# A state-space block in four layers: B, C and the step sizes of a segment out of one projection instead of two

## The chip, the cores and the metric

The kernel runs on one core of one Trainium2 chip. The metric is the time of one execution on the device, in microseconds (us); 19,610.8 us is the median of three runs of the kernel before. Engines are named as in the profile: PE is TensorE (PEld its weight loads), DVE is VectorE, ACT is ScalarE, POOL is GpSimd, SP is the engine from which all transfers (DMAs) are issued.

## The reference, cut to what matters

Four images of 64x64 tokens with 96 channels pass through four layers, each a mixer and a feed-forward part with a residual each. The mixer of layer 0 is a gated recurrence. Those of layers 1 to 3 are selective scans, and the change concerns them alone. For each image and layer:

```python
x_dbl = jnp.einsum('bkdl,kcd->bkcl', xs, x_proj_weight)        # k: 4 orders, d: 192 channels
dts, Bmat, Cmat = jnp.split(x_dbl, [DT_RANK, DT_RANK + D_STATE], axis=2)   # 6, 16 and 16 rows
dts = jnp.einsum('bkrl,kdr->bkdl', dts, dt_projs_weight)
delta = jax.nn.softplus(dts + dt_projs_bias[None, :, :, None])
# for each state n of 16, along the 4096 tokens:
dA = jnp.exp(dl[..., None] * A)
h = dA * h + (dl * u_l)[..., None] * b_l[:, :, None, :]
y = jnp.einsum('bkdn,bkn->bkd', h, c_l)
```

B, C and the step sizes (`dts`) of a token are three slices of one matrix product of the scan's input with `x_proj_weight`. The 4096 tokens are scanned in four orders: by rows and by columns, each forwards and backwards.

## The kernel before, in words

**Stages.** After layer 0, 12 stages follow: layers 1 to 3, and in each the four images. A stage takes one image through one layer's scans: 2 directions x 4 segments of 1024 tokens (T) x 3 chunks of 128 channel rows (two orders share a chunk, 64 partitions each) x 16 states n. One (chunk, state) of one segment is a **scan tile**; a segment has 48 tiles, a stage 384, the whole 4608. Positions below are given as chunk (first, second, third) and tile n (0 to 15), or as the tile's number in its stage.

**One scan tile** (`scans`, from line 873). ACT makes `da` = exp(delta x A). PE spreads row n of B over the channel rows by multiplying `bs` with a selector (`b_rows`, line 917: `bc<-bs,sel`, two matmuls into one of two double PSUM banks). DVE multiplies `bc` by `du`, in place in PSUM, and scans (`scan`, line 926). POOL multiplies the result `h` by the C row (`times_c`, line 948); the C row was read from DRAM by a DMA that repeats it over 64 partitions (`c_rows`, line 901: `c<-cs`, issued two tiles ahead). PE sums over the states (`add_quarters`, line 953: `acc<-c,twice`, eight matmuls) three tiles later. Each engine works through its instructions in the order in which the program issues them; the class `InOrder` records that order, which is why every instruction of the profile carries line 78.

**B in three parts.** `bs` is bf16 with 96 partitions: 0 to 31 hold B rounded to bf16, 32 to 63 the rounded remainder, 64 to 95 what the second rounding leaves. The selector adds up the three.

**Preparing a segment** (`prepare_segment`, line 775; 96 times). For each half k of 512 tokens, three matmuls (one per chunk of `u`) project onto 108 rows in one PSUM bank, `x_proj_b`: three copies of the 32 rows of B (two orders x 16 states) and, from row 96 on (NB3), the 12 rows of step sizes. ACT copies the step sizes to `rows` and casts all 96 B rows to `bs`; DVE subtracts `bs` from the bank into `rows[0:96]`; ACT casts the remainder to partitions 32 to 63 and 64 to 95 of `bs`. When both halves are done, POOL makes the last part in one instruction. After that the C rows are projected by themselves, again three matmuls per half, into a bank `x_proj_c`; ACT copies each to `rows[0:32]`, and SP stores them to `cs` in DRAM, where `c_rows` finds them.

**The planner.** Beside the scan tiles, three kinds of work are laid into the program as generators ("chains"), each `yield` ending a turn:

- the chunk chain, `prepare_chunk` of the next chunk (line 824): four passes over `dt_proj` banks, softplus on ACT and POOL; it starts at n = 0 of each chunk;
- the segment chain, `next_segment` (line 863): load `u`, wait two turns, then `prepare_segment` for the next segment; it starts at n = 4 of the second chunk;
- the jobs (`Job`, line 717; `between`, line 623): what lies between two layers for the next stage's image, namely the joining of the four orders, the output projection, the feed-forward part, the input projection and the convolution, in eight strips each.

Each scan tile gives one turn to the chunk chain, then one to the segment chain, and then as many turns to the job as its credit allows (1.65 per tile, line 1317; 2.6 for the last layer's jobs). These turns are issued between a tile's multiply and its scan (`beside`, line 1033). A turn that needs a PSUM bank announces it (`yield True`), and `pump` (line 136) refuses it when neither of the two single banks is free; a bank counts as free again from the next tile on. At n = 13 what is left of a chain is run out. A job that is not done at tile 356 of its stage (line 1022) is run out there with no scans beside it.

The weights of both projections lie in one array, XPW columns for each direction and chunk (lines 40 and 297); `_scan` fills it on the host (lines 1365 to 1376).

Of the kernel before, what the change touches and what calls it, by code (L numbers as in the profile page):

```python
# [15 lines left out]
ALU = mybir.AluOpType  # L16
# [5 lines left out]
NS = 16  # L22
DI = 192
R = 6
HID = 4 * C
T = 1024
MM = 512
# [9 lines left out]

NB3 = 96
NC2 = 2 * NS
XPW = NB3 + 2 * R + NC2  # L40
W_IN = 0
W_OUT = W_IN + 6 * 128
W_CW = W_OUT + 2 * C
# [5 lines left out]
W_XP = W_LN + 4  # L49
W_SSM = W_XP + 6 * XPW  # L50

# [48 lines left out]
def metaformer(ctx: ExitStack, tc: tile.TileContext, x, l0_ab, l0_rest, ssm, ffn, out):  # L100
    nc = tc.nc
    pe, act, dve, pool, sp = (
        InOrder(tc, e) for e in (nc.tensor, nc.scalar, nc.vector, nc.gpsimd, nc.sync)
    )
# [6 lines left out]
    def sb(bufs, tag, shape, dtype=F32):  # L111
        return pools[bufs].tile(shape, dtype, tag=tag, name=tag)

    def const(name, shape, dtype=F32):
        return pools[1].tile(shape, dtype, name=name)
# [9 lines left out]
    def bank(name):  # L125
        banks["free"] -= 1
        return banks["pool"].tile([128, MM], F32, tag="ps", name=name)

    def release():
        banks["back"] += 1  # L130
# [31 lines left out]
    for k in range(2):  # L162
        p = slice(64 * k, 64 * k + 64)
# [31 lines left out]
    for layer in range(4):  # L195
# [8 lines left out]
        b = const(f"b_{layer}", [128, 3 + C])  # L204
# [72 lines left out]
    class Weights:  # L277
# [17 lines left out]
        def load_xp(self):  # L295
            if self.xp is None:
                self.xp = sb(1, "xp", [128, 6 * XPW])
                sp.dma_start(out=self.xp, in_=ssm[self.layer - 1, :, W_XP:W_SSM])
# [476 lines left out]
    def prepare_segment(item, sg):  # L775

        xp = weights[item.layer].xp
        m = NB3 + 2 * R

        def project(ps, a, b, k):  # L780

            for c in range(3):
                o = (3 * item.d + c) * XPW
                cols = slice(k * MM, (k + 1) * MM)
                pe.matmul(
                    ps[0 : b - a],
                    xp[:, o + a : o + b],
                    sg.us[c][:, cols],
                    start=c == 0,
                    stop=c == 2,  # L790
                )
                if c:
                    yield

        sg.rows = sb(1, "rows", [128, T])
        for k in range(2):
            cols = slice(k * MM, (k + 1) * MM)
            ps = bank("x_proj_b")
            yield from project(ps, 0, m, k)

            bs = sg.bs[:, cols]
            act.copy(sg.rows[NB3:m, cols], ps[NB3:m])
            sg.steps = k == 1
            act.copy(bs, ps[0:NB3])
            yield
            rem = sg.rows[0:NB3, cols]
            dve.tensor_tensor(rem, ps[0:NB3], bs, ALU.subtract)
            release()
            yield
            for p in (32, 64):  # L810
                act.copy(bs[p : p + 32], rem[p : p + 32])
            yield k == 0
        pool.tensor_tensor(sg.bs[64:96], sg.rows[64:96], sg.bs[64:96], ALU.subtract)
        for k in range(2):
            cols = slice(k * MM, (k + 1) * MM)
            yield True
            ps = bank("x_proj_c")
            yield from project(ps, m, m + NC2, k)
            act.copy(sg.rows[0:NC2, cols], ps[0:NC2])
            release()  # L820
        yield
        sp.dma_start(out=sg.cs, in_=sg.rows[0:NC2])

    def prepare_chunk(item):

# [37 lines left out]
    def next_segment(items):  # L863

        sg = load_segment(items[0])
        for i in items:
            i.sg = sg
        yield
        yield
        yield True  # L870
        yield from prepare_segment(items[0], sg)

    def scans(stages, jobs, pac):
# [11 lines left out]
        for i in items[:3]:  # L885
            i.sg = sg
        drain(Chain(prepare_segment(items[0], sg), True))
        drain(Chain(prepare_chunk(items[0]), True))
        tiles = [(i, n) for i in items for n in range(NS)]
# [417 lines left out]
    with tc.tile_pool(name="pbig", bufs=2, space=bass.MemoryType.PSUM) as wides_pool:  # L1307
        wides.append(wides_pool)
        with tc.tile_pool(name="pl0", bufs=1, space=bass.MemoryType.PSUM) as pl0:
            gated(images, Job(between(images[0], 0), 2.6, patience=1), pl0)  # L1310
        stages = [(im, layer) for layer in range(1, 4) for im in images]
        jobs = []
        for at in range(len(stages)):
            jobs.append([])
            if at + 1 < len(stages):
                im, layer = stages[at + 1]
                jobs[-1].append(Job(between(im, layer - 1), 1.65))

            for im in {10: images[:2], 11: images[2:3]}.get(at, ()):
                jobs[-1].append(Job(between(im, 3, im.dst), 2.6))  # L1320
        with tc.tile_pool(name="pac", bufs=1, space=bass.MemoryType.PSUM) as pac:
            scans(stages, jobs, pac)
# [31 lines left out]
def _chunks(v):  # L1354

    v = v.reshape(2, 2, DI, -1)
    v = [np.concatenate([v[:, o, c : c + 64] for c, o in halves], 1) for halves in CHUNKS]
    return np.stack(v, 1).transpose(2, 0, 1, 3)


def _scan(in_w, conv_w, conv_b, xp_w, dt_w, dt_b, A_logs, Ds, ln_w, ln_b, out_w):
    w = np.zeros((128, W_SSM), np.float32)
    twice = np.r_[128:DI, 128:DI]

    xp = np.zeros((128, 2, 3, XPW), np.float32)
    m = NB3 + 2 * R
    for d in range(2):
        for chunk, halves in enumerate(CHUNKS):
            for k, (ch, order) in enumerate(halves):
                t = xp_w[2 * d + order].T[ch : ch + 64]  # L1370
                v = xp[64 * k : 64 * k + 64, d, chunk]
                for s in range(3):
                    v[:, 32 * s + NS * order : 32 * s + NS * order + NS] = t[:, R : R + NS]
                v[:, NB3 + R * order : NB3 + R * order + R] = t[:, :R]
                v[:, m + NS * order : m + NS * order + NS] = t[:, R + NS :]
    w[:, W_XP:W_SSM] = xp.reshape(128, -1)
    t = in_w.T
    w[:C, W_IN : W_IN + 448] = np.concatenate([t[:, :128], t[:, twice], t[:, DI:]], 1)
    dt = np.zeros((2 * R, 2, 3, 128), np.float32)
    for d in range(2):  # L1380
        for chunk, halves in enumerate(CHUNKS):
            for k, (ch, order) in enumerate(halves):
                t = dt_w[2 * d + order].T
                dt[R * order : R * order + R, d, chunk, 64 * k : 64 * k + 64] = t[:, ch : ch + 64]
    w[NB3 : NB3 + 2 * R, W_IN:W_OUT] = dt.reshape(2 * R, -1)
    w[:, W_OUT : W_OUT + C] = out_w.T[:128]
    w[:64, W_OUT + C : W_CW] = out_w.T[128:]
    taps = conv_w.reshape(DI, 9)
    w[:, W_CW : W_CW + 9] = taps[:128]
    w[:64, W_CW + 9 : W_CB] = np.concatenate([taps[128:, 0:3], taps[128:, 6:9]], 1)  # L1390
    w[64:, W_CW + 9 : W_CW + 12] = taps[128:, 3:6]
    w[:, W_CB:W_DTB] = np.stack([conv_b[:128], conv_b[twice]], 1)
    w[:, W_DTB:W_AL] = _chunks(dt_b[..., None]).reshape(128, -1)
    w[:, W_AL:W_DS] = _chunks(A_logs.reshape(4, DI, NS)).reshape(128, -1)
    w[:, W_DS:W_LN] = _chunks(Ds.reshape(4, DI, 1)).reshape(128, -1)
    w[:, W_LN : W_LN + 2] = np.stack([ln_w[:128], ln_b[:128]], 1)
    w[:64, W_LN + 2 : W_XP] = np.stack([ln_w[128:], ln_b[128:]], 1)
    return w
# [46 lines left out]
```

## Time and profile before

| | |
|---|---|
| median of three runs | 19,610.8 us (19,587.3 to 19,634.2) |
| profiled execution | 19,605.7 us; span of its instructions 19,603.9 us |
| mean granted TensorE clock | 0.816 of full speed |
| layer 0 and start | to 1802 us of the span |
| scan tiles | 1802 to 19,384 us |
| six C matmuls' group `x_proj_c`, 1152 in all | 657.8 us of PE, 687 ns mean |
| copies of C out of PSUM, 192 | 107.5 us of ACT, 560 ns mean |
| subtract `rows<-x_proj_b,bs`, 96x512, 192 | 130.1 us of DVE, 677 ns mean |
| `cs<-rows` stores, 96 | 4.6 us to landing (median) |

How to read it: a group's line names line, engine, operation, output<-inputs, shapes and count, then busy time and the mean of one, then the idle time of that engine just before these instructions and what ended most of it. `DVE bc <- PE bc` in the waits means that DVE stood before an instruction writing `bc` until PE's instruction writing `bc` was done. Busy shares of different engines overlap in time.

### The profile page before, as it was taken

To read this page: it belongs to the slowest core of one execution; us is meant where nothing else is said; L and a number is where in the kernel's file an instruction comes from. 1 tells how busy PE (TensorE), PEld (TensorE's weight loads), DVE (VectorE), ACT (ScalarE), POOL (GpSimd) and SP (SyncE) were. 2 spreads that over 40 slices of the span, in tenths; PEclk is the share of its full clock that TensorE was granted. 3 is DMA by queue.
4 is the path that set the end of the run, shared out by engine and by line. 5 is a ranking of instruction groups with operands and counts; after the bars stand their busy time and mean duration, and the time that the engine had idled before them with its cause. 6 is when DMAs were issued, how large, how long until landed. Compare 5 with 4: busy or idle time off the path is not lost. (4 is left out here: it accounts for less than half of the span.)

```text
span 19603.9 us, 224830 instructions
## 1 busy us (share of the span) xinstructions
PE 16279.3 (83%) x70400; PEld 4745.4 (24%) x70400; DVE 17669.3 (90%) x13768; ACT 12248.8 (62%) x19341; POOL 15496.4 (79%) x10086
## 2 busy tenths in 40 slices
PE   8998787787888888887888887887888888888877
PEld 3332121121122222222222222222222222223223
DVE  6757999999999999999999999999999999998885
ACT  4544665665665665675665665665675665666665
POOL 3435888888888888888888888888888888888886
PEclk9998786787787787797797797797797797797776
DMA  2213666676666666667666667666666666676664
GB/s 52 50 47 89 166 184 168 168 188 166 169 186 172 170 182 180 167 185 182 169 183 180 167 182 183 167 182 182 168 186 178 168 185 176 171 185 171 168 177 115
DMA packets 1269876, 3192.65 MB, mean 163 GB/s; under 512 B 440336, under 2 KB 440560, under 8 KB 1262544
## 3 DMA queue, kind: packets, MB, share of 16 engines
q1 hardware_dynamic: 1268688, 3178.27, 61.6%
q8 instruction: 568, 9.31, 0.2%
q14 instruction: 620, 5.08, 0.1%
HBM read 2818.81 MB, written 308.28 MB: 160 GB/s over the span
## 5 line engine op out<-in xcount | busy, mean ns | idle before, releaser
L78 POOL TENSOR_TENSOR c<-h,c 128x1024 f32<-128x1024 f32 (+1 forms) x4992 | 11332.9, 2276 | 3284.9 <-DVE h L78 1396.4
L78 DVE TENSOR_TENSOR_SCAN h<-da,carry,bc 128x1024 f32<-128x1024 f32 x4608 | 10797.5, 2343 | 598.7 <-POOL c L78 80.8
L78 PE MATMUL acc<-c,twice 64*64 64x512 f32 x36864 | 6246.6, 755 | 57.4 <-POOL c L78 57.4
L78 ACT ACTIVATE da<-delta,decay 128x1024 f32<-128x1024 f32 x4608 | 5280.8, 1148 | 1372.5 <-DVE h L78 1359.7
L78 DVE TENSOR_TENSOR bc<-du,bc 128x1024 f32<-128x1024 f32 x4608 | 5567.1, 1208 | 417.8 <-PE bc L78 389.6
L78 PE MATMUL bc<-bs,sel 96*128 96x512 bf16 x9216 | 3398.6, 457 | 2393.3 <-DVE h L78 2296.6
L78 ACT COPY carry<-h 128x1 f32<-128x1 f32 x3456 | 649.1, 188 | 2997.7 <-DVE h L78 2992.8
L78 PEld LDWEIGHTS <-sel 96*128 96x128 bf16 x9216 | 557.0, 101 | 7376.4 <-DVE h L78 5607.2
L78 PEld LDWEIGHTS acc<-c,twice 64*64 64x64 f32 x36864 | 1131.3, 153 | 2848.4 <-issue 1927.6
L78 ACT ACT_TABLE_LOAD x1165 | 1494.7, 1283 | 36.3 <-DVE mv L78 20.0
L78 PE MATMUL conv<-pad,tap_lo 128*128 128x512 f32 x1728 | 913.5, 639 | 0.6 <-ACT zh L78 0.6
L78 PE MATMUL dt_proj<-rows,w 12*128 12x512 f32 x1152 | 829.5, 807 | 6.3 <-ACT delta L78 6.3
L78 ACT ACTIVATE du<-e,ones 128x1024 f32<-128x1024 f32 x576 | 659.4, 1145 | 202.9 <-POOL delta L78 197.8
L78 POOL TENSOR_TENSOR delta<-delta,du 128x1024 f32<-128x1024 f32 x288 | 679.2, 2358 | 121.7 <-ACT du L78 121.3
L78 PE MATMUL x_proj_c<-u,xp 128*32 128x512 f32 x1152 | 657.8, 687 | 133.2 <-ACT rows L78 125.0
L78 PE MATMUL x_proj_b<-u,xp 128*108 128x512 f32 x1152 | 696.1, 722 | 53.7 <-ACT u L78 12.8
L78 ACT COPY y<-acc 128x1024 f32<-128x1024 f32 x288 | 291.3, 1012 | 713.8 <-PE acc L78 708.9
L78 POOL TENSOR_TENSOR e<-e,du 128x1024 f32<-128x1024 f32 x288 | 679.7, 2360 | 2.4 <-ACT du L78 2.4
L78 POOL TENSOR_TENSOR du<-delta,u 128x1024 f32<-128x1024 f32 x288 | 680.0, 2361 | 0.1
L78 POOL TENSOR_TENSOR delta<-delta,e 128x1024 f32<-128x1024 f32 x288 | 678.7, 2357 | 0.1
L78 ACT ACTIVATE c<-c,l_bias 128x512 f32<-128x512 f32 x384 | 263.6, 686 | 662.6 <-PE c L78 659.8
L78 PE MATMUL conv<-pad,tap_hi 128*128 128x512 f32 (+1 forms) x1152 | 598.8, 621 | 3.8 <-ACT u L78 3.8
(152 smaller groups left out, 15323.9 us busy)
## 6 DMA issues: line engine op xcount, KB each, us to landing
c<-cs SPq DMA_DIRECT2D x9216, 256.0 KB, 4.2
u<-u SPq DMA_DIRECT2D x288, 512.0 KB, 6.8
y<-y SPq DMA_DIRECT2D x1152, 128.0 KB, 3.5
y<-y SPq DMA_DIRECT2D x144, 512.0 KB, 6.4
xr<-x SPq DMA_DIRECT2D x224, 192.0 KB, 5.1
u<-u SPq DMA_DIRECT2D x288, 128.0 KB, 2.7
pad<-y SPq DMA_DIRECT2D x288, 128.0 KB, 5.1
z<-zl SPq DMA_DIRECT2D x96, 256.0 KB, 3.4
```

What stands on the lines that cost most here:

```text
L78: ins = f(*a, **k).ins
```

## The change

One projection per half in place of two. Its 108 rows are now: B (0 to 31), C (32 to 63), 32 rows of zero weights (64 to 95), and the step sizes at 96 to 107 as before. ACT copies all 108 rows to `rows` and casts only 32 rows of B to `bs`. DVE subtracts those 32 rows of `bs` from the bank's first 32 and writes the remainder to `rows[64:96]`. ACT casts the remainder twice, as before. SP's store of C now reads `rows[32:64]` and is issued right after the second half, ahead of POOL's subtract. The second loop with its two banks is gone. The job rate goes from 1.65 to 1.6 turns per tile.

```diff
-XPW = NB3 + 2 * R + NC2
+XPW = NB3 + 2 * R
...
-        sg.rows = sb(1, "rows", [128, T])
+        rows = sg.rows = sb(1, "rows", [128, T])
         for k in range(2):
             cols = slice(k * MM, (k + 1) * MM)
-            ps = bank("x_proj_b")
-            yield from project(ps, 0, m, k)
-
+            ps = bank("x_proj")
+            for c in range(3):
+                o = (3 * item.d + c) * XPW
+                pe.matmul(
+                    ps[0:XPW], xp[:, o : o + XPW], sg.us[c][:, cols], start=c == 0, stop=c == 2
+                )
+                if c:
+                    yield
             bs = sg.bs[:, cols]
-            act.copy(sg.rows[NB3:m, cols], ps[NB3:m])
+            act.copy(rows[0:XPW, cols], ps[0:XPW])
             sg.steps = k == 1
-            act.copy(bs, ps[0:NB3])
+            act.copy(bs[0:32], ps[0:32])
             yield
-            rem = sg.rows[0:NB3, cols]
-            dve.tensor_tensor(rem, ps[0:NB3], bs, ALU.subtract)
+            rem = rows[64:96, cols]
+            dve.tensor_tensor(rem, ps[0:32], bs[0:32], ALU.subtract)
             release()
             yield
             for p in (32, 64):
-                act.copy(bs[p : p + 32], rem[p : p + 32])
+                act.copy(bs[p : p + 32], rem)
             yield k == 0
-        pool.tensor_tensor(sg.bs[64:96], sg.rows[64:96], sg.bs[64:96], ALU.subtract)
-        for k in range(2):
-            cols = slice(k * MM, (k + 1) * MM)
-            yield True
-            ps = bank("x_proj_c")
-            yield from project(ps, m, m + NC2, k)
-            act.copy(sg.rows[0:NC2, cols], ps[0:NC2])
-            release()
-        yield
-        sp.dma_start(out=sg.cs, in_=sg.rows[0:NC2])
+        sp.dma_start(out=sg.cs, in_=rows[NC2 : 2 * NC2])
+        pool.tensor_tensor(sg.bs[64:96], rows[64:96], sg.bs[64:96], ALU.subtract)
...
-                jobs[-1].append(Job(between(im, layer - 1), 1.65))
+                jobs[-1].append(Job(between(im, layer - 1), 1.6))
...
-                for s in range(3):
-                    v[:, 32 * s + NS * order : 32 * s + NS * order + NS] = t[:, R : R + NS]
+                v[:, NS * order : NS * order + NS] = t[:, R : R + NS]
+                v[:, NC2 + NS * order : NC2 + NS * order + NS] = t[:, R + NS :]
                 v[:, NB3 + R * order : NB3 + R * order + R] = t[:, :R]
-                v[:, m + NS * order : m + NS * order + NS] = t[:, R + NS :]
```

## The prediction

> **What bounds the kernel now.** I read the page's busy lines first, then the groups of instructions.
>
> ```profile
> PE 16279.3 (83%) x70400; PEld 4745.4 (24%) x70400; DVE 17669.3 (90%) x13768; ACT 12248.8 (62%) x19341; POOL 15496.4 (79%) x10086
> ...
> PEclk9998786787787787797797797797797797797776
> ```
>
> ```profile
> L78 DVE TENSOR_TENSOR_SCAN h<-da,carry,bc 128x1024 f32<-128x1024 f32 x4608 | 10797.5, 2343 | 598.7 <-POOL c L78 80.8
> L78 DVE TENSOR_TENSOR bc<-du,bc 128x1024 f32<-128x1024 f32 x4608 | 5567.1, 1208 | 417.8 <-PE bc L78 389.6
> ...
> L78 PE MATMUL x_proj_c<-u,xp 128*32 128x512 f32 x1152 | 657.8, 687 | 133.2 <-ACT rows L78 125.0
> L78 PE MATMUL x_proj_b<-u,xp 128*108 128x512 f32 x1152 | 696.1, 722 | 53.7 <-ACT u L78 12.8
> ```
>
> DVE is the bound: each of 4608 scan tiles costs it one multiply (1208 ns) and one scan (2343 ns), 16,365 us in all, and the tiles run from 1802 to 19,384 us of the span. The change leaves those two alone. What can be won is DVE's idle time there. From the trace I took the distance from each multiply to the next and subtracted DVE's own other work between them. An undisturbed tile then takes about 3.56 us (1.208 + 2.343 and the seams), and all that lies above 3.56, over all tiles, is **429 us**. That is the most that any change of waits can bring. The waits say who causes it.
>
> ```profile
> DVE bc L78 <- PE bc L78: 389.6, 271, 5.1
> ...
> PEld x_proj_c L78 <- ACT rows L78: 157.9, 67, 4.9
> ...
> PE x_proj_c L78 <- ACT rows L78: 125.0, 65, 4.5
> ```
>
> Columns: total us, times, longest. The multiply waits for its operand `bc` from TensorE, 390 us in all. TensorE works in order, and the third projection (`x_proj_c`) is where it stands before ScalarE. The timeline of one case (columns: start us, duration, engine):
>
> ```profile
> 8635.58 0.56 ACT L78 COPY rows<-x_proj_c 32x512 f32<-32x512 f32 x1
> ...
> 8636.19 1.90 PE L78 MATMUL x_proj_c<-u,xp 128*32 128x512 f32 x4 [2.00 <-ACT rows L78]
> ...
> 8639.08 1.09 PE L78 MATMUL acc<-c,twice 64*64 64x512 f32 x8
> ...
> 8640.10 0.61 PE L78 MATMUL bc<-bs,sel 96*128 96x512 bf16 x2
> ...
> 8640.75 1.23 DVE L78 TENSOR_TENSOR bc<-du,bc 128x1024 f32<-128x1024 f32 x1 [1.41 <-PE bc L78]
> ```
>
> ScalarE comes late to empty a C bank (it had a table load and two passes of the next chunk's softplus ahead of it); TensorE stands 2.00 us; the matmuls behind it move back; DVE idles 1.41 us.
>
> To price this by place I summed the excess over 3.56 us by position in a segment (three chunks of 16 tiles). In tiles 2 to 9 of the three chunks it is 1.75, 0.47 and **1.91 us per segment** (96 segments); the other 24 positions together have 0.35. The C projection lies in tiles 2 to 8 of the third chunk. The first chunk's 1.75 holds 12 intervals at the starts of stages, where POOL waits up to 10.77 us for a `c<-cs` load behind the big loads of a new job; without them it is 1.68.
>
> **What the Trainium skill says.** "VectorE: DVE Perf Modes", section "Two Vector instructions with no wait between them": a Vector instruction whose output starts in another group of 32 partitions than the last output into that memory starts only after all earlier ones have finished. The trace agrees: of the four 64-partition COPYs that build `twice`, the second and fourth start 77 and 82 ns before the end of the one ahead; the third, which moves to partition 64, starts 13 ns after it. "TensorE: Matmul & The Clock Gate", section "LDWEIGHTS (loading the stationary operand)": a load's time goes with its columns; the medians agree, 175 ns for 108 and 109 ns for 32, while the matmuls take 594 and 593 ns. So 108 columns in one projection cost what 108 do now. Same page, Part 1: the clock falls to half after an idle window. The trace has half clock in 37% of the tiles, but 11% in tiles 4 to 7 of the third chunk, where C keeps TensorE busy.
>
> **The change, part by part**, for 96 segments.
>
> *Removed: six C matmuls, two ScalarE copies (558 ns each), two bank uses and seven turns of the segment's chain.* TensorE loses 658 us and ScalarE 107 us of busy time; neither counts as such, only what DVE waits. In tiles 2 to 9 of the third chunk the 1.91 us become what a chunk has with softplus and job but no C. The two neighbours are the nearest rows: 0.47 and 1.68. I take their mean, 1.08: (1.91 - 1.08) x 96 = **-80 us**. The ends are 0.47 (-138 us) and 1.68 (-22 us). The cover is not free: a bank that C does not hold goes to a job. By following the planner's rule (one turn of each chain per tile, a turn refused when no bank is free) through the code, counting turns and no times, jobs take 244 banks in those tiles now and 299 after, against 294 in the first chunk now. That is why I do not take 0.47. The half clock that a less busy TensorE gets is inside this substitution too.
>
> *The subtract, 192 of it, now reads partitions 0 to 31 and writes 64 to 95.* Its row is 96x512 at 677 ns; with 512 elements per partition as before I take 677 ns again. But it changes the output's partition group, and so does the scan behind it (`h` starts at 0). Now the subtract starts 91 ns before the multiply's end and the scan 80 ns before the subtract's. Each becomes +13 ns by the COPY row: 104 + 93 = 197 ns, x192 = **+38 us**, straight on DVE. It can't be a gain: the same elements, one instruction for one. Lower end 0, if none is held; upper end +54, if it also takes as long as DVE's slowest 512-element row with a PSUM operand (759 ns; 82 ns x192 = 16 us). It must now follow the rows copy as well, but waits for the later cast anyway (45 us in 17 waits now, the scan queued behind): no new wait.
>
> *The rows copy takes 108 partitions instead of 12, the cast 32 instead of 96*: 579 and 582 ns for 12 and 96 partitions now, so 0. The two casts of the remainder (616 ns) and POOL's 2124 ns subtract stay, in the same turn.
>
> *The `cs` store is issued about seven turns earlier and ahead of POOL's subtract.* SP's queue is in order; the store waits only for the two rows copies, some turns old by then, and the first reader is issued at tile 14 of the third chunk, so nothing waits for it: 0. Were the copy late, the `c` loads queued behind it would wait, and then POOL; they are issued two tiles ahead.
>
> *The first segment is prepared before any scan, uncovered.* ScalarE's first `e` starts at 1783.01 us, and its last cast before that ends at 1780.37; without C it can follow it: **-3 us**. The smaller `xp` load (648 columns for 840) saves at most part of the one 9 us wait for it: 0 to -2, taken as 0.
>
> *The job rate 1.65 to 1.6.* The count of turns puts the job's last step at tile 289 (stages 0 to 2), 345 (3 and 7) and 337 (the others), and the trace has the `u` stores there, at 290, 345 and 338. The deadline is tile 356: a job not done by then is run out with the scans standing. With both edits the last step comes at 298, 339 and 328, so there is no run-out; refused turns fall from about 165 to 103 per stage. In the last stage three jobs end at tile 333 instead of 373. The work is the same: 0. But every job step now meets other scan steps. Stages 4, 5, 6, 8 and 9 have one schedule and excesses of 22.7 to 36.2 us, so a new schedule may well move a stage by 5 us, and eight stages alike: +-40 us, for the range.
>
> **Sum:** -80 + 38 - 3 = **-45 us** on the profiled execution's 19605.7 (span 19603.9). The median of the three runs, 19,610.8, lies 5 us above it; -45 gives 19,566, rounded **19,565 us**. About 0.2% (39 us) is what a measurement of this kernel can tell from no change.
>
> **The rivals.**
> 1. *C's place stays free* (as in the second chunk, 0.47): -138 + 38 - 3 = -103, 19,508 us. For it: the longest waits name C. Against: jobs take the banks.
> 2. *The gain goes to the jobs and the hold*: the third chunk becomes like the first: -22 + 38 - 3 = +13, 19,624 us, no change. For it: 299 bank uses against 294. Against: in stages 0 to 2 the third chunk has 2.24 where the first has 1.48 and the second 0.61.
> 3. *Slower: the freed bank makes it worse.* Heavier job matmuls (a group of nine `conv` at 639 ns is 5.8 us, against 4.1 us for six of C) stand ahead of `bc` in tiles 2 to 9 of the third chunk, in the same ScalarE congestion. With 2.24 us there, stages 0 to 2's own figure, the change is +32 + 38 - 3 = +67, 19,678 us. It decides from 1.95 us on: then 4 + 38 - 3 is +39. For it: 55 bank uses in that window come back as the jobs'. Against: C's six matmuls and its ScalarE copies go, and the tiles in which two banks are taken fall from 370 to 333.
> 4. *It doesn't do what it says*, as when the framework orders the subtract or the store behind more than the code asks; the writes are to separate columns or partitions, so I give it no share of its own.
>
> **How the numbers follow.** Forecast 38%, rival 1 20%, rival 2 22%, rival 3 20%. Of the forecast some 4 points fall within 0.2%: faster 0.54, same 0.26, slower 0.20. The range reaches down past rival 1 with most of the schedule's 40 us (19,470) and up to most of rival 3 (19,660), leaving out about 8% and 10%.
>
> **What would show it.** `x_proj_c` gone with its two waits (283 us). DVE <- PE `bc` at some 300 us instead of 390. Excess in tiles 2 to 9 of the third chunk near 1.1 us per segment. The subtract at 677 ns, starting just after the multiply's end. Clock share slightly lower, job ends at 298, 339 and 328. It is wrong if that excess stays above 1.95 us, if the subtract takes notably longer than 677 ns, or if excess turns up in the first two chunks.

## The result, and the profile after

The changed kernel takes **19,406.6 us** (median of 4 runs, 19,400.0 to 19,414.0), the kernel before on the same chip 19,611.6 us: a ratio of **0.9894** with a 95% interval of 0.988 to 0.9909, or 205 us less. The prediction had the sign right (19,565 us), but the time lies 63 us below the low end of its range. The profiled execution's span went from 19,603.9 to 19,402.3 us (-201.6), at a mean TensorE clock of 0.801 (0.816 before).

The page of the changed kernel, the lines that answer to those of before:

```profile
PE 15935.0 (82%) x69248; PEld 4652.0 (24%) x69248; DVE 17697.8 (91%) x13768; ACT 12105.6 (62%) x19150; POOL 15479.3 (80%) x10086
...
PEclk9998796786786797797797797797797797788775
...
L78 DVE TENSOR_TENSOR_SCAN h<-da,carry,bc 128x1024 f32<-128x1024 f32 x4608 | 10798.3, 2343 | 567.9 <-POOL c L78 63.3
...
L78 DVE TENSOR_TENSOR bc<-du,bc 128x1024 f32<-128x1024 f32 x4608 | 5569.1, 1209 | 287.4 <-PE bc L78 264.7
...
L78 PE MATMUL x_proj<-u,xp 128*108 128x512 f32 x1152 | 706.2, 731 | 31.4 <-ACT u L78 12.4
```

Scan and multiply cost DVE what they did. The multiply's idle time before it fell from 417.8 to 287.4 us, and what TensorE's `bc` causes of it from 389.6 to 264.7 us. One `x_proj` group of 706 us stands in place of two with 1354 us. The waits of DVE (total us, times, longest us):

```profile
DVE bc L78 <- PE bc L78: 264.7, 232, 6.3
...
DVE rows L78 <- ACT bs L78: 36.6, 17, 14.5
```

The subtract waits for ScalarE's cast as often as before (17 times; 45.3 us then). So the rows copy that it must now follow is no new wait.

The excess over 3.56 us per tile, counted as in the prediction, fell from 429 to 223 us: **-206**. DVE's other work between the multiplies grew by 7.5 us, the first multiply starts 2.0 us earlier and the tail is 0.9 us shorter: -206 + 7.5 - 2.0 - 0.9 = -201.4, the span's -201.6. By place (us per segment of 48 tiles, 96 segments):

| place | before | after | us in all |
|---|---|---|---|
| tiles 2-9 of the first chunk | 1.75 | 0.68 | -103 |
| tiles 2-9 of the second chunk | 0.47 | 0.23 | -23 |
| tiles 2-9 of the third chunk | 1.91 | 1.05 | -82 |
| where the subtracts are (second chunk from tile 10, third to tile 1) | -0.22 | 0.06 | +27 |

The third chunk did what was forecast (-80). What was not forecast is the first chunk, which has none of the edited instructions in it, and the second. Something reached the whole schedule.

### The profile page after: what moved, and what is told of

Same layout as the page of the kernel before. It is cut to its first block, busy times and chain, and to the rows that moved or that the text cites. A ratio compares the mean times of both kernels' runs of the same rounds, so it can differ in the third digit from the quotient of the medians.

```text
span 19402.3 us, 222370 instructions
## 1 busy us (share of the span) xinstructions
PE 15935.0 (82%) x69248; PEld 4652.0 (24%) x69248; DVE 17697.8 (91%) x13768; ACT 12105.6 (62%) x19150; POOL 15479.3 (80%) x10086
## 5 line engine op out<-in xcount | busy, mean ns | idle before, releaser
L78 PE MATMUL acc<-c,twice 64*64 64x512 f32 x36864 | 6385.9, 770 | 39.2 <-POOL c L78 39.1
L78 DVE TENSOR_TENSOR bc<-du,bc 128x1024 f32<-128x1024 f32 x4608 | 5569.1, 1209 | 287.4 <-PE bc L78 264.7
L78 PE MATMUL bc<-bs,sel 96*128 96x512 bf16 x9216 | 3486.1, 468 | 2663.6 <-DVE h L78 2562.1
L78 PE MATMUL x_proj<-u,xp 128*108 128x512 f32 x1152 | 706.2, 731 | 31.4 <-ACT u L78 12.4
L78 DVE TENSOR_TENSOR_SCAN h<-da,l_carry,bc 128x512 f32<-128x512 f32 x384 | 491.4, 1280 | 42.4 <-DVE bc L78 1.8
```

What stands on the lines that cost most here:

```text
L78: ins = f(*a, **k).ins
```

## The experiments

Three theories. **Work**: the gain comes from the six C matmuls and two copies that are gone. **Turns**: it comes from the turns and bank uses that they held, which jobs now get. **Pace**: it comes from the job rate, 1.6 for 1.65, which decides which job step meets which scan step all through the kernel. The prediction rests on Work with a share of Turns, and puts Pace at 0.

To read the traces I split the excess in two: "late" is tiles 345 to 383 of every stage but the last (the end of the jobs and the change of stage), "rest" is all other tiles. Before: rest 396, late 34 us. After: rest 198, late 26.

**The pace taken alone, both ways.** `e1_rate_165` is the changed kernel, `e2_before_rate_160` the kernel before, each with the other's rate:

```diff
 e1, from the kernel after
-                jobs[-1].append(Job(between(im, layer - 1), 1.6))
+                jobs[-1].append(Job(between(im, layer - 1), 1.65))
 e2, from the kernel before
-                jobs[-1].append(Job(between(im, layer - 1), 1.65))
+                jobs[-1].append(Job(between(im, layer - 1), 1.6))
```

> The changed kernel with the old job rate of 1.65. Three theories of the 126 us that came from outside the third chunk's tiles 2 to 9, where none were forecast. Work: C's matmuls and copies slow DVE wherever they stand, so the rate is nothing: 19,390 to 19,430 us. Banks and turns: what helps is that the segment's chain holds two banks less and the jobs are refused less often; that is so at 1.65 too: 19,390 to 19,440 us. Pace: it is how the job's steps happen to fall on the scan tiles, and 1.6 was a good draw; at 1.65 much of the 126 us is lost: 19,470 to 19,550 us.

> The kernel before with the job rate of 1.6 alone. Work, or banks and turns: 1.6 brings nothing by itself, 19,590 to 19,640 us, the few steps that are run out at tile 356 of two stages among it. Pace: the slower rate thins out the jobs' steps, and a large part of the 126 us is had without touching the projection: 19,480 to 19,550 us.

Measured: e1 **0.9944** (0.9932 to 0.9956; 19,525 us against 19,629), e2 **1.0023** (1.0014 to 1.0033; 19,674 us). e1 lies in the range given for Pace, e2 in neither range. At the old pace, then, a little over half of the gain is left; at the new pace the old kernel loses. It looks as if the pace were worth nothing without the projection, but the trace of e2 splits: rest **259** us (-137), late **208** us (+175). The slower job saves 137 us in the middle of the stages (133 of it before tile 300, so it isn't work that was only put off to the end) and loses more at their ends. Another 23 us come after the last multiply (243 us to the end for 220 before), where 120 `ff_y` matmuls are left to do for 96. One end of a stage, in the timeline of e2 (start us, duration, engine; idle time before it and its releaser in brackets):

```profile
8907.63 1.73 SPq L78 DMA_DIRECT2D u<-u  x3
...
8910.75 4.89 SPq L78 DMA_DIRECT2D u<-part_c  x2
...
8915.73 5.05 SPq L78 DMA_DIRECT2D c<-cs  x2
...
8920.24 2.35 DVE L78 TENSOR_TENSOR_SCAN h<-da,carry,bc 128x1024 f32<-128x1024 f32 x1
8921.11 3.79 SPq L78 DMA_DIRECT2D u<-u  x3
...
8929.98 3.93 PE L78 MATMUL x_proj_b<-u,xp 128*108 128x512 f32 x4 [14.20 <-DMA u<-u]
...
8933.84 1.98 PE L78 MATMUL acc<-c,twice 64*64 64x512 f32 x8
...
8935.75 0.61 PE L78 MATMUL bc<-bs,sel 96*128 96x512 bf16 x2
...
8936.39 1.23 DVE L78 TENSOR_TENSOR bc<-du,bc 128x1024 f32<-128x1024 f32 x1 [13.80 <-PE bc L78]
```

The job is not done by tile 356, so what is left of it is run out there: in SP's order its last stores of `u` (from 8907.63 us) and of the two reordered copies (`u<-cols_a`, `u<-part_c`) stand behind the `y` stores of tile 355 and ahead of the `c<-cs` loads that tile 356 issues. The expectation had that for two stages; the trace has it in all eight, 3 to 10. The next segment's load of `u` stands behind all these and starts at 8921 us, at tile 360; in the kernel before it starts at tile 356 in this stage. The projection of that segment is next in TensorE's queue and stands 14.2 us for the load; `acc` and `bc`, which need no `u`, stand behind it, and DVE loses 13.8 us. It comes back in each of the eight stages, with up to 18.8 us; together these are 120 of the 208 us. The changed kernel at 1.6 ends its jobs at tiles 328 and 336 in these stages and has late 26 us.

**The projection without the turns.** `e3_turns_kept` has the one projection, but the segment's chain still spends the turns and bank counts that C's two halves took, the store of C keeps its old place, and the rate is 1.65: all else is issued in the order of before. `e8_turns_kept_160` is the same at 1.6.

```diff
-        sp.dma_start(out=sg.cs, in_=rows[NC2 : 2 * NC2])
         pool.tensor_tensor(sg.bs[64:96], rows[64:96], sg.bs[64:96], ALU.subtract)
+        for k in range(2):
+            yield True
+            banks["free"] -= 1
+            yield
+            yield
+            release()
+        yield
+        sp.dma_start(out=sg.cs, in_=rows[NC2 : 2 * NC2])
...
-                jobs[-1].append(Job(between(im, layer - 1), 1.6))
+                jobs[-1].append(Job(between(im, layer - 1), 1.65))
```

> The single projection at rate 1.65, but the segment's chain still takes the turns of the two C halves and counts a bank as taken in them, without a matmul or a copy; C is stored when they are over, as before. The order of all other work on every engine is then that of the kernel before. Work: nearly all of the gain stays, 19,400 to 19,450 us. Banks and turns, and pace too: only the third chunk's gain less the shifted subtract stays (82 - 46 us): 19,560 to 19,590 us.

> At rate 1.6, the single projection while the segment's chain keeps the turns and the bank count of the two C halves: the order of everything else is that of the kernel before at 1.6, which measured 1.0023 of the kernel before. If C's own work is worth 100 us whatever the order (as at 1.65, where this kernel measured 0.9947): ratio 0.995 to 0.9985 (19,530 to 19,600 us), and the rest of the changed kernel's gain is the new order at 1.6. If the gain from 1.65 to 1.6 comes with C's work gone, in any order: 0.988 to 0.991.

Measured: e3 **0.9947** (0.9933 to 0.996; 19,529 us), not to be told from e1. e8 **0.9989** (0.9981 to 0.9998; 19,599 us against 19,621). Neither lies in a range that was given: e3 is between its two, e8 just above the higher of its two. The waits of DVE in e3:

```profile
DVE bc L78 <- PE bc L78: 278.7, 197, 5.1
```

and in e1:

```profile
DVE bc L78 <- PE bc L78: 336.1, 242, 6.1
```

Step by step from before to after, the rest excess by place (us in all; late tiles left out, which is why the third chunk's first number is below 1.91 x 96):

| | first chunk 2-9 | second 2-9 | third 2-9 | at the subtracts | elsewhere | rest | late |
|---|---|---|---|---|---|---|---|
| before, 1.65 | 155 | 38 | 176 | -18 | 45 | 396 | 34 |
| e3: projection, turns kept, 1.65 | 157 | 40 | 68 | 13 | 54 | 332 | 30 |
| e1: turns freed, 1.65 | 100 | 66 | 113 | 33 | 16 | 327 | 28 |
| after: 1.6 | 65 | 19 | 92 | 3 | 19 | 198 | 26 |

These are single executions: e1's profiled one lies 13 us above its median, that of before 23 us below the median of before that was measured beside e1. So a step's size is good to some 30 us, and the steps from before to e3 and to e1 come out short by about that. By the ratios the projection with its turns is worth 0.56 points and the pace 0.50, some 110 and 98 us; by the rest excess 69 and 130.

What each step shows:

- *Work* (before to e3): the idle time leaves the third chunk (-108), the subtract's places take 31 back, the first two chunks don't move. Net -64 in these two executions, 100 by the medians. What the matmuls are worth of it and what the copies isn't separated.
- *Turns* (e3 to e1): freed turns move idle time about (third chunk +45, subtracts +20, second chunk +26; first chunk -57, elsewhere -38) and sum to -5. That fits the prediction's count, in which jobs take C's place; it did not see that as much is saved elsewhere. C's earlier store is in this step too.
- *Pace* (e1 to after): -130, most of it in the first and second chunks.

The pace's share is nearly the same in three pairs: before to e2 396 to 259 (-137), e3 to e8 332 to 197 (-135), e1 to after 327 to 198 (-130). The first two pairs share one order of the jobs' turns, and their saving is alike in place too, most of it in the first chunk: 155 to 55 and 157 to 51 us. So these are two orders, not three, and two that agree make no rule, as the other rates below show. e8, with C's turns still held, has late 214 us, which is the collision shown in e2. So Turns earns nothing measurable in the rest and still matters: with the turns freed, a job at 1.6 ends before its deadline, and 214 becomes 26.

**The shifted subtract.** `e4_no_shift` writes the remainder to `rows[0:32]`, on the partitions that the subtract reads, and ScalarE makes the one copy at 64 that POOL needs. It was run twice (`e16_no_shift_again`).

```diff
-            rem = rows[64:96, cols]
+            rem = rows[0:32, cols]
             dve.tensor_tensor(rem, ps[0:32], bs[0:32], ALU.subtract)
...
                 act.copy(bs[p : p + 32], rem)
+            act.copy(rows[64:96, cols], rem)
```

> The changed kernel with the remainder written to partitions 0 to 31 of rows, where the subtract's inputs start too, and copied from there to 64 to 95 by one more ScalarE copy per half, for POOL. If the seams of the shifted subtract cost DVE what they show (122 and 112 ns more than before, 192 times, 45 us): 19,350 to 19,375 us, with 108 us more on ScalarE hidden. If those seams are hidden elsewhere: 19,400 to 19,415 us. If the ScalarE copies come in DVE's way as C's did: above 19,415 us.

> The remainder written to partitions 0 to 31, as in e4, once more. If the shift's 31 to 35 us at the subtract's places are a gain that stays: 0.987 to 0.989, as in e4 (0.9883), against 0.9894 twice for the changed kernel. If e4 was only a good set of runs: 0.989 to 0.9905.

Measured: 0.9883 (0.9869 to 0.9896) and 0.989 (0.9876 to 0.9903), against 0.9894 (0.988 to 0.9907) for the changed kernel run again (`e5_changed_again`): the intervals overlap. e4 lies where the seams would be hidden elsewhere; e16 lies on the border of its two ranges and decides nothing. The seams did come back. DVE's timeline in the kernel after, one subtract between multiply and scan:

```profile
8165.05 1.21 DVE L78 TENSOR_TENSOR bc<-du,bc 128x1024 f32<-128x1024 f32 x1
...
8166.29 0.68 DVE L78 TENSOR_TENSOR rows<-x_proj,bs 32x512 f32<-32x512 f32 x1
...
8167.01 2.35 DVE L78 TENSOR_TENSOR_SCAN h<-da,carry,bc 128x1024 f32<-128x1024 f32 x1
```

and in the kernel before:

```profile
8050.85 1.21 DVE L78 TENSOR_TENSOR bc<-du,bc 128x1024 f32<-128x1024 f32 x1
...
8051.96 0.68 DVE L78 TENSOR_TENSOR rows<-x_proj_b,bs 96x512 f32<-96x512 f32 x1
...
8052.56 2.33 DVE L78 TENSOR_TENSOR_SCAN h<-da,carry,bc 128x1024 f32<-128x1024 f32 x1
```

Before, the subtract starts ahead of the multiply's end (8050.85 + 1.21 = 8052.06) and the scan ahead of the subtract's; after, each starts when the one ahead has ended. Medians: -91 and -79 ns before, +31 and +33 ns after, -92 and -71 ns in e4. With 6 ns more for the instruction itself that is 240 ns for each of 192, **46 us**. The excess at the subtracts' places fell by 33 us in e4 and 27 us in e16, as it should. But the third chunk rose by 16 and 30 us and the second by 16 and 11; part of that is scatter, since the third chunk of e5, the same kernel as after, has 12 us more than that of after. DVE's waits in e4:

```profile
DVE bc L78 <- PE bc L78: 303.6, 256, 6.3
```

against 264.7 us after; e16 has 308.8 and e5 270.4. So with either pair the multiply stands some 38 us longer for `bc`, about what the subtract no longer costs. e4 has 192 more ScalarE copies, so ScalarE's new work and the earlier DVE aren't separated here. A version without the extra copy, with POOL reading the remainder at partition 0, was not tried. What is shown is that taking the shift away in this way gains nothing measurable.

**Is 1.6 a good pace, or a good throw?** Here are the changed kernel and the kernel before at other rates, and the changed kernel with the job's credit starting at another value than 0, which shifts all job steps of a stage by a part of a tile and leaves the rate alone (shown for 0.3; `e14_start_06` has 0.6, `e15_start_05_at_165` has 0.5 at 1.65):

```diff
-            self.rounds, self.rate, self.credit = rounds, rate, 0.0
+            self.rounds, self.rate, self.credit = rounds, rate, 0.3 if rate < 2 else 0.0
```

> The changed kernel itself, as the yardstick for the others on one chip: ratio to the kernel before 0.988 to 0.991 by every theory (19,400 to 19,450 us).

> The changed kernel at rate 1.55. The job is then done by tile 345 at the latest, so nothing is run out. Draw (each rate is one more throw of how job steps fall on scan tiles, 1.6 a good one, without a trend): 19,450 to 19,570 us. Thinner is better (a slower rate spreads the jobs, which the freed banks have made possible): 19,360 to 19,410 us.

> The changed kernel at rate 1.7. Draw: 19,450 to 19,570 us, and not in order with 1.55, 1.6 and 1.65. Thinner is better: above 1.65, 19,550 to 19,620 us.

> The kernel before with job rate 1.7: the job's last step comes at tile 326 to 331, so nothing is late at the stage's end. If rates are draws in the old projection too: ratio 0.994 to 1.006, either side. If a higher rate is worse by itself, as from 1.65 to 1.7 in the changed kernel (0.9944 to 0.9999): 1.003 to 1.008.

> The changed kernel at 1.625, between its 0.9894 at 1.6 and its 0.9944 at 1.65. Draw: anywhere from 0.989 to 0.998, with stalls at other tiles than at 1.6 and 1.65. Smooth (something about a rate near 1.6 is good): 0.990 to 0.993.

> The changed kernel at 1.61, a hair from 1.6. Draw: 0.990 to 0.998, since a turn that falls one tile later moves all that follow. Smooth: 0.988 to 0.991, as at 1.6.

> The changed kernel at 1.575, between its 0.9951 at 1.55 and its 0.9894 at 1.6. Its job's last step comes at tile 354 in two stages and 346 in the others, so some of the next segment's loads may come late (e2 lost 13.8 us per stage at tile 360 with last steps at 349 and 356). Draw: 0.990 to 0.998 and up to 0.2% of lateness. Smooth: 0.990 to 0.993 and the lateness.

> The changed kernel at rate 1.6 with every 1.6 job's credit starting at 0.3 instead of 0: the same turns per tile, the same pattern of two turns in three tiles of five, begun one tile later in the pattern. By the rule the job's last step then comes at tile 351 or 346 instead of 339 or 328. If 1.6 is a good rate whatever falls where: 0.988 to 0.991 of the kernel before, plus up to 0.1% of lateness at tile 360. If 1.6 from 0 was a good throw: 0.992 to 0.998.

> The same with the credit starting at 0.6; last steps at tile 337 or 328, as in the changed kernel, so nothing is late. Good rate: 0.988 to 0.991. Good throw: 0.992 to 0.998.

> The changed kernel at rate 1.65 with the credit starting at 0.5; last steps at 328 and 322. If 1.65 is the worse rate: 0.9935 to 0.9955, as from 0 (0.9944). If each start is a throw: anywhere from 0.989 to 0.999, and not near 0.9944 by need.

The kernel before took 19,621 us beside e5 to e8 and 19,626 us beside e9 to e16.

| run | kernel, rate, start | ratio to before (95%) | median us | rest | late |
|---|---|---|---|---|---|
| e6_rate_155 | after, 1.55 | 0.9951 (0.9937 to 0.9965) | 19,525 | 322 | 57 |
| e12_rate_1575 | after, 1.575 | 0.9909 (0.9896 to 0.9923) | 19,452 | 219 | 44 |
| e5_changed_again | after, 1.6 | 0.9894 (0.988 to 0.9907) | 19,413 | 205 | 26 |
| e13_start_03 | after, 1.6, 0.3 | 0.9926 (0.9914 to 0.9939) | 19,487 | 264 | 54 |
| e14_start_06 | after, 1.6, 0.6 | 0.9924 (0.9912 to 0.9936) | 19,481 | 261 | 30 |
| e11_rate_161 | after, 1.61 | 0.9937 (0.9924 to 0.995) | 19,509 | 305 | 54 |
| e10_rate_1625 | after, 1.625 | 0.9923 (0.991 to 0.9935) | 19,474 | 282 | 20 |
| e1_rate_165 | after, 1.65 | 0.9944 (0.9932 to 0.9956) | 19,525 | 327 | 28 |
| e15_start_05_at_165 | after, 1.65, 0.5 | 0.9962 (0.9948 to 0.9975) | 19,561 | 359 | 29 |
| e7_rate_170 | after, 1.7 | 0.9999 (0.9991 to 1.0007) | 19,616 | 403 | 25 |
| e9_before_rate_170 | before, 1.7 | 0.9989 (0.9982 to 0.9996) | 19,601 | 403 | 32 |

Of the ranges given, 1.55 fell in that of Draw and 1.7 in that of Thinner, so neither theory had both. 1.61 and the two other starts at 1.6 fell on the side of the throw, and so did 1.7 in the kernel before. 1.65 from 0.5 lies above what a worse rate was to give, though its interval reaches that; 1.575 and 1.625 don't decide.

One edit of 0.01 in the rate (1.6 to 1.61) costs 0.43 points of ratio, four fifths of what the projection is worth in e3; a start shifted by 0.3 or 0.6 costs 0.3. In 1.61 and in the start at 0.3, 28 us of the loss (0.14 points) lie in the late tiles; the start at 0.6 has nearly nothing there (30 us for 26) and loses its 0.3 in the rest. So the exact schedule can make more than half of the 0.5 points between 1.65 and 1.6. Perhaps not all of it: the three starts at 1.6 (198 to 205, 264, 261 us of rest excess) lie below the two at 1.65 (327, 359), and 1.7 is the worst rate for the changed kernel. Five throws can't say more. And at 1.7 the new projection shows nothing: 0.9999 against 0.9989 for the old one, rest 403 and 403. The gain of the edit depends on the schedule that it is put into.

What makes one schedule good was not found. The traces show the form only: in stages 3 to 9 of the kernel before, single collisions of 1.5 to 5 us come back at the same tiles (6, 40, 104, 218, 296, 97) of stage after stage. After the change tiles 6 and 40 still have theirs, 104, 218, 296 and 97 have not, 39 and 255 are new, and there are fewer: 94 tiles outside the late ones have an excess above 1.5 us, 164 before.

## Why the prediction was wrong

| step | forecast, us | measured, us |
|---|---|---|
| third chunk, tiles 2-9 | -80 | -82 |
| shifted subtract | +38 | 46 by the seams; +31 at its places with the order kept (e3), +27 after |
| first segment's start | -3 | -2 |
| rows copy, cast, early store of C | 0 | copy and cast 564 and 569 ns (579 and 582 before); no new wait |
| job rate 1.65 to 1.6 | 0, +-40 for the range | **-130** in the changed kernel (98 by the ratios), -135 and -137 in the two others, by the traces outside the late tiles |
| sum | -45 | -205 |

**The step that failed** is "*The job rate 1.65 to 1.6* ... The work is the same: 0", with its bound: "a new schedule may well move a stage by 5 us, and eight stages alike: +-40 us". The work is the same, and that says nothing of the idle time. The bound came from the spread of stages 4, 5, 6, 8 and 9, which share one schedule. It measures how much a stage varies at a fixed schedule, not how far another schedule lies away. Measured in the pair before to e2, stages 0 to 10 together lost 132 us of rest excess (297 to 165): 12 us each, ten down by 6 to 21 us and one up by 0.4. The one other schedule in view would not have given it either: in stages 0 to 2, which have their own, the three chunks had 1.48, 0.61 and 2.24 us against 1.68, 0.47 and 1.91 over all (the first chunk without the first segments of the stages). By sign that is 0.27 us more per segment, or 26 us in 96 segments.

**The third chunk: right in size, by some luck.** The number is a sum of three. C's work gone is worth -108 us there (e3, near rival 1's "C's place stays free"), the freed turns give 45 back (e1), which fits the prediction's count of 299 bank uses by jobs for 244, and the pace takes 22 again. That the neighbours' mean hit -82 owes something to the last term, which it did not contain.

**The subtract: right mechanism, small miss.** The rule that the prediction took from the Trainium skill ("VectorE: DVE Perf Modes", section "Two Vector instructions with no wait between them") holds here: both seams turned from overlap to a gap. The price from the COPY row (+13 ns) was low; here it is +31 and +33 ns. e4 took the gaps away and won nothing measurable of the whole; the multiply's wait is longer there instead.

**The rest of what would show it:** `x_proj_c` and its 283 us of waits are gone; the clock is lower; the job's `u` stores stand at tiles 295, 336 to 337 and 328 to 329 (298, 339 and 328 forecast); `bc` waits 265 us where 300 was forecast (at the old pace, in e1, 336). The projection's matmuls cost what 108 rows did before (731 ns in the mean for 722). The weight loads that the prediction cites, 175 ns for 108 columns and 109 for 32, grow with the columns but not in proportion; nothing hangs on that here. The sign of being wrong, that "excess turns up in the first two chunks", came the other way round: excess left them.

**The rivals.** Rival 1 (C's place stays free, 0.47 us in the third chunk) is what e3 comes near to with 0.72, but with the turns freed it is 1.27 in e1. Rival 2 (all goes to the jobs and the hold) needs 1.68 in the third chunk; at 1.6 it has 1.05. At rate 1.7, where nothing of the gain is left, rival 2 isn't the cause either: the third chunk has 54 us there, and the first two have 126 and 123. Rival 3 (the freed bank makes it worse) needs 1.95 or more there, and neither 1.05 nor 1.27 comes near.

**The projection by itself** was under-sized as well. Without the rate step the forecast is the same -45 us; e1, which is that kernel, is 67 us shorter than the kernel before by the two profiled spans (19,536.5 and 19,603.9) and 104 us by the medians (19,525 and 19,629). At the places that the forecast names, e1 gives -63 in the third chunk and +51 at the subtracts, -12 where -80 and +38 make -42. The other 56 us are what it did not contain, what the freed turns do in the rest of the segment: first chunk -55, second +28, elsewhere -29.

**What stays open:** why 1.6 starting at 0 suits this kernel; whether another pair of rate and start does better; and whether the subtract's 46 us can be had without a copy on ScalarE. No version tried is faster than the changed kernel beyond its interval.

## What to carry to other kernels

In a kernel that interleaves background work by a fixed pace, an edit of one step can also be an edit of the schedule, and a change of pace can't be priced at 0 because the work is the same. Run the old and the new code at several paces and starts before an edit is credited, and put into the range the spread between schedules, not that between stages of one schedule. Freed turns may earn nothing in the steady part and still decide whether a slower pace meets its deadline, so ask of a pace both what it saves in the middle and what then comes late at the end.

## What the runs showed of the hardware

- A subtract of 32 partitions x 512 from PSUM takes 682 ns when it writes to another group of partitions and 669 ns when it doesn't, against 677 ns for 96 partitions: a third of the partitions saves 8 ns at most. The group of the kernel before, that of the kernel after, and that of e4:

```profile
L78 DVE TENSOR_TENSOR rows<-x_proj_b,bs 96x512 f32<-96x512 f32 x192 | 130.1, 677 | 45.5 <-ACT bs L78 45.3
```

```profile
L78 DVE TENSOR_TENSOR rows<-x_proj,bs 32x512 f32<-32x512 f32 x192 | 131.0, 682 | 41.9 <-ACT bs L78 36.6
```

```profile
L78 DVE TENSOR_TENSOR rows<-x_proj,bs 32x512 f32<-32x512 f32 x192 | 128.5, 669 | 34.1 <-ACT bs L78 34.1
```

- The price of the other group is in the seams: 122 and 112 ns more than before on the subtract's two sides, and back to overlap in e4.
- TensorE has less to do and gets a lower clock (half clock in 41% of the scan tiles' time for 37%, mean 0.801 for 0.816), and the kernel is faster all the same. The mean clock was no guide to the time here.
